# A graph attention and mixture-of-experts kernel: rows of x for 48 edge tiles fetched ahead of the table, edge lists loaded in rows

## The chip, the cores and the metric

The kernel runs on one core of one Trainium2 chip. The metric is the device time of one execution in microseconds (us). Four runs of the kernel before took 2566.82 to 2573.57 us, with a median of 2571.59 us.

## What is computed

There are 6250 nodes with 256 features and 206250 edges (two directions of 100000 random pairs, and one self-loop a node), sorted by destination. The first layer is graph attention with 8 heads of 32 features, the second a mixture of 16 experts, of which each node uses two.

```python
xn = layernorm(x)
hh = (xn @ W).reshape(n, 8, 32)
scores = leaky_relu((hh*a_src).sum(-1)[src] + (hh*a_dst).sum(-1)[dst], 0.2)
alpha = exp(scores - segment_max(scores, dst)[dst]);  alpha /= segment_sum(alpha, dst)[dst]
out = segment_sum(hh[src] * alpha[:, :, None], dst) + xn
x = x + elu(layernorm(out) * gamma + beta)
x = x + layernorm(y + moe(y)) * f_gamma + f_beta          # y = layernorm(x), top 2 of 16 experts
```

## The kernel before, in words

**The table.** The kernel first makes a table in DRAM with one row of 280 floats for every node: 8 heads of 32 features and a one each (264 floats), then two factors of the attention weight for each head (16 floats). x is held in 49 blocks of 128 nodes, all loaded ahead by SP (xs, L159) in batches of 2, 6, 8, 8, ... blocks. For each block TensorE turns the block (L294), ScalarE copies it out of PSUM (L296), TensorE multiplies it by W with the attention vectors folded in (wx, L299), ScalarE scales the product and takes two exponentials (L302 to L309), VectorE keeps the scores (sd, L310), and POOL stores the block's rows (L313). The normalization's statistics are VectorE's (L193, L194).

**The edge lists.** src and dst are cut into 52 chunks of 31 tiles of 128 edges (NK, CT). Before, edge e of a chunk stands on partition e // 31, in column e % 31, so that each partition reads 124 contiguous bytes for each chunk (L129 to L141). windows() (L242), traced ahead of the seventh batch, subtracts the first destination of a chunk from its destinations (dl), turns dl in 13 pieces on TensorE, which ScalarE casts to bytes (dlt, L260) and SP stores (dlb, L261), and takes the bounds of the distances.

**The edge loop.** The loop runs over the chunks, and in each over four groups of 8, 8, 8 and 7 tiles (GROUPS). For each tile POOL issues one indirect DMA that gathers 128 table rows by the source indices into a buffer hx (gather, L200 to L211). There are four such buffers of one group each. The first two groups are gathered right after the table (L316). For each group VectorE makes two matrices of zeros and ones (ohT L1022, oh L1029); TensorE multiplies ohT by the destinations' factors (pm, L1040); VectorE forms the weights (uv, L1064 to L1069) and multiplies the gathered rows by them (L1072); TensorE sums the rows into the chunk's destinations (agg, L1076). At the end of a chunk the sum is carried over (L1090 to L1095) and stored to accd, and a block of 128 finished nodes goes through node_block (L584): it loads a from accd and x, normalizes, applies the ELU, writes rest (L620) and computes the routing's logits (lg, L630).

**The experts.** When a round of blocks is complete (ROUNDS, five of them), routing() places its rows, POOL scatters every block's row twice (L830, out of ys, L816), and expert tiles of 128 rows are worked one per group, three groups (LAG) after the scatters: weights are loaded by SP, and TensorE multiplies (L881, L896). After the loop the open tiles are worked, and the results are fetched (L915), combined, normalized and stored.

**Order of work.** A scheduler puts each engine's instructions in a fixed order, by the place in the program and by estimated times. tc.issue_after(i) puts the block's instructions behind i on i's engine alone. Every engine works its own queue in order. POOL's queue holds the table stores, the gathers, the scatters and the result fetches; SP's holds the loads and some of the stores.

Of the kernel before, what the change touches and what calls it, by code (L numbers as in the profile page):

```python
# [36 lines left out]
def kernel(  # L37
# [89 lines left out]
    tp, tr = tail // CT, tail % CT  # L127

    def edge_list(eng, t, ap):  # L129
        eng.dma_start(  # L130
            t[:, : (NK - 1) * CT].rearrange("p (k g) -> p k g", g=CT),
            ap[0 : (NK - 1) * CE].rearrange("(k p g) -> p k g", p=P, g=CT),
        )
        o = (NK - 1) * CE
        if tp:
            eng.dma_start(t[:tp, (NK - 1) * CT : NT], ap[o : o + tp * CT].rearrange("(p g) -> p g", g=CT))
        if tr:
            eng.dma_start(
                t[tp : tp + 1, (NK - 1) * CT : (NK - 1) * CT + tr],
                ap[o + tp * CT : NE].rearrange("(p g) -> p g", p=1),  # L140
            )  # L141

    hxp = ctx.enter_context(tc.tile_pool(name="hxp", bufs=4))
    prep = ctx.enter_context(ExitStack())
    ed = prep.enter_context(tc.tile_pool(name="ed", bufs=1))
    dst_i = ed.tile([P, NT], I32, name="dst_i")
    nc.vector.memset(dst_i[:, (NK - 1) * CT :], N - 1)
    nc.vector.memset(src_sb[:, (NK - 1) * CT :], PADN)
    nc.vector.memset(src_sb[:, NT:], PADN)
    xs = ed.tile([P, NB, C], F32, name="xs")  # L150
    nc.vector.memset(xs[:, NB - 1, :], 0.0)
    batches = []
    while not batches or batches[-1][1] < NB:
        i = batches[-1][1] if batches else 0
        batches.append((i, min(NB, i + (2, 6, 8)[min(2, len(batches))])))
    for i, j in batches:
        n = min(j, NB - 1) - i
        if n:
            nc.sync.dma_start(xs[:, i : i + n, :], x[i * P : (i + n) * P, :].rearrange("(i p) c -> p i c", p=P))  # L159
    nc.sync.dma_start(xs[:LAST, NB - 1, :], x[(NB - 1) * P : N, :])  # L160
    wx = ed.tile([P, KC, C + 2 * H], F32, name="wx")
# [6 lines left out]
    nc.sync.dma_start(base_i[:, : NK - 1], dst[0 : (NK - 1) * CE].rearrange("(k e) -> e k", e=CE)[0:1, :])  # L168
    nc.sync.dma_start(base_i[:, NK - 1 :], dst[(NK - 1) * CE : (NK - 1) * CE + 1].rearrange("(k e) -> e k", e=1))
    edge_list(nc.sync, dst_i, dst)  # L170
    edge_list(nc.sync, src_sb, src)

# [5 lines left out]
    gg = row_of(g_gamma, C, "gg")  # L178
    gb = row_of(g_beta, C, "gb")
    fg = row_of(f_gamma, C, "fg")  # L180
    fb = row_of(f_beta, C, "fb")
    gtb = row_of(gate_b, E, "gtb")
    gw = const.tile([P, KC, E], F32, name="gw")
    nc.sync.dma_start(gw, gate_w.rearrange("(k p) e -> p k e", p=P))


    rest = const.tile([P, NB, C], F32, name="rest")
# [12 lines left out]
    def gather(k, g0, n):  # L200

        hx = hxp.tile([P, n, R], F32, name="hx")
        for g in range(n):
            c = k * CT + g0 + g
            t = nc.gpsimd.indirect_dma_start(  # L205
                out=hx[:, g, :],
                out_offset=None,
                in_=table[:, :],
                in_offset=bass.IndirectOffsetOnAxis(ap=src_sb[:, c : c + 1], axis=0),
            )  # L210
        return hx, t  # L211
# [5 lines left out]
    with tc.tile_pool(name="a1", bufs=1) as a1, tc.tile_pool(name="a3", bufs=3) as a3, tc.tile_pool(  # L217
        name="aps", bufs=4, space=bass.MemoryType.PSUM
    ) as aps:
# [22 lines left out]
        def windows():  # L242

            base_f = a1.tile([1, NK], F32, name="base_f")
            nc.vector.tensor_copy(base_f, base_i)
            bb = aps.tile([P, NK], F32, name="pxt")
            nc.tensor.matmul(bb, lhsT=ones[:1, :], rhs=base_f, start=True, stop=True)
            base_b = a1.tile([P, NK], F32, name="base_b")
            nc.vector.tensor_copy(base_b, bb)
            nc.vector.tensor_sub(down[:, : NK - 1], base_b[:, : NK - 1], base_b[:, 1:])  # L250
            nc.vector.tensor_copy(dl, dst_i)
            d3 = dl.rearrange("p (k g) -> p k g", g=CT)
            nc.vector.tensor_tensor(d3, d3, base_b[:, :, None].to_broadcast([P, NK, CT]), ALU.subtract)

            dlt = a1.tile([P, TR, P], U8, name="dlt")
            for i in range(TR):
                n = min(P, NT - i * P)
                pt = aps.tile([P, P], F32, name="pxt")
                nc.tensor.transpose(pt[:n, :], dl[:, i * P : i * P + n], ident)
                nc.scalar.copy(dlt[:n, i, :], pt[:n, :])  # L260
                nc.sync.dma_start(dlb[i * P : i * P + n, :], dlt[:n, i, :])  # L261
            b1r = a1.tile([E, F], F32, name="b1r")
            nc.scalar.dma_start(b1r, b1)
            b1t = a1.tile([P, E, FC], F32, name="b1t")
            for f in range(FC):
                pt = aps.tile([P, E], F32, name="pxt")
                nc.tensor.transpose(pt, b1r[:, f * P : (f + 1) * P], ident[:E, :E])
                nc.vector.tensor_copy(b1t[:, :, f], pt)
            nc.scalar.dma_start(b1d.rearrange("e p f -> p e f"), b1t)
            two = a1.tile([P, 2], F32, name="two")  # L270
            nc.vector.tensor_reduce(two[:, 0:1], dl, AX.X, ALU.max)
            nc.vector.tensor_reduce(two[:, 1:2], dl, AX.X, ALU.min)
            nc.vector.tensor_scalar(two[:, 1:2], two[:, 1:2], -1.0, float(P - 1), op0=ALU.mult, op1=ALU.add)
            pw = aps.tile([2, P], F32, name="pxt")
            nc.tensor.transpose(pw, two, ident)
            far = a1.tile([2, 1], F32, name="far")
            nc.vector.tensor_reduce(far, pw, AX.X, ALU.max)
            pf_ = a1.tile([1, 2], F32, name="pf_")
            pp = aps.tile([1, 2], F32, name="ph")
            nc.tensor.transpose(pp, far, ident[:2, :2])  # L280
            nc.vector.tensor_copy(pf_, pp)
            return base_f, pf_

        for q, (i0, i1) in enumerate(batches):
            if q == 6:
                base_f, pf_ = windows()
            for b in range(i0, i1):
                stats(a3, xs[:, b, :], st[:, b, :])
            inv_std(rstd[:, i0:i1], st[:, i0:i1, 1])
            nc.vector.tensor_scalar_mul(low[:, i0:i1], rstd[:, i0:i1], 0.2)  # L290
            for b in range(i0, i1):
                pt = aps.tile([P, KC, P], F32, name="pxt")
                for k in range(KC):
                    nc.tensor.transpose(pt[:, k, :], xs[:, b, k * P : (k + 1) * P], ident)  # L294
# [18 lines left out]
                nc.gpsimd.dma_start(table[b * P : (b + 1) * P, :], hr)  # L313


# [78 lines left out]

    def load(ap, lo_, hi_, engines=mybir.ALL_ENGINES, after=()):
# [8 lines left out]
    with tc.If(load(flag[:, 0:1], 0, 1) > 0):  # L404
        with tc.tile_pool(name="m1", bufs=1) as m1, tc.tile_pool(name="m2", bufs=2) as m2, tc.tile_pool(
# [6 lines left out]
            nc.vector.tensor_copy(dst_f[:, :NT], dst_i)  # L412
# [148 lines left out]
    with tc.tile_pool(name="w2", bufs=2) as w2_, tc.tile_pool(name="w3", bufs=3) as w3_, tc.tile_pool(  # L561
# [252 lines left out]
        def to_send(b):  # L814

            y = e2.tile([P, C], F32, name="ys", bufs=5)  # L816
# [227 lines left out]

        weighed = []
# [5 lines left out]
        for k in range(NK):  # L1051
            after = used[-2] if k > 1 else ()
            agg = wps.tile([P, RA], F32, name="agg")
            for g0, n in BOUNDS:
# [4 lines left out]
                hx, gathered = early.pop(0) if early else gather(k, g0, n)  # L1059
# [24 lines left out]
                some()  # L1084
                if g0 == 0:
# [96 lines left out]
```

## Time and profile before

| | us |
|---|---|
| median of 4 runs | 2571.59 (2566.82 to 2573.57) |
| the profiled execution | 2573.83 |
| its span, from the first to the last instruction | 2572.0 |
| first table store, last table store issued by POOL | 18.1, 87.9 |
| first and last table gather issued by POOL | 90.5, 2241.2 |
| POOL busy in gathers of the table, 1612 of them | 1543.0 |
| POOL busy in scatters and in result fetches, 98 each | 97.1, 97.1 |
| POOL busy in table stores, 49 | 26.7 |
| mean granted TensorE clock | 0.857 |

A busy time counts the instruction on its engine; the DMA that it starts moves its data later, and the wait for that stands with the instruction that needs the data. "Idle before" is the time in which an engine did nothing ahead of an instruction, and the releaser is what ended it. Durations are those of one execution under the profiler.

### The profile page before, as it was taken

What the parts mean: (1) busy time and instruction counts of PE and PEld (TensorE: products, weight loads), DVE (VectorE), ACT (ScalarE), POOL (GpSimd) and SP (SyncE); (2) the same over time, 40 slices, a digit from 0 to 9 for tenths busy, and PEclk for the clock granted to TensorE, in tenths of its full rate; (3) what the DMA queues carried; (4) which work ended last, traced back from release to release, by engine and by line L of the source; (5) the groups of instructions that cost most, each with busy time, mean ns of one, the idle gap of its engine ahead of it and who ended that gap; (6) DMA issues with size and microseconds to landing.
All of it is one profiled execution on the core that took longest, in us unless ns stands there. A gap on an engine that the chain in (4) does not pass through costs nothing.

```text
span 2572.0 us, 34571 instructions
## 1 busy us (share of the span) xinstructions
PE 1847.5 (72%) x10229; PEld 1552.4 (60%) x10229; DVE 1608.3 (63%) x3120; ACT 526.6 (20%) x1822; POOL 1765.0 (69%) x1866
## 2 busy tenths in 40 slices
PE   7365665655662679889847888867889868868985
PEld 6244454444451568778736777756778657756774
DVE  5476666666674666766747676665766846747802
ACT  6200000000000122222211222212222212224442
POOL 3577777777777777777777777777777777747202
PEclk9677778777876899899979999888889989979997
DMA  7555556555445588898857888877888878849995
GB/s 222 134 147 170 151 161 173 152 170 141 131 139 156 161 245 269 270 282 264 270 173 238 247 275 272 266 236 248 262 264 278 249 232 263 281 150 337 300 289 164
DMA packets 389306, 567.74 MB, mean 221 GB/s; under 512 B 102535, under 2 KB 278750, under 8 KB 389110
## 3 DMA queue, kind: packets, MB, share of 16 engines
q0 software_dynamic: 89904, 263.85, 34.6%
q1 hardware_dynamic: 257130, 264.89, 33.7%
q10 hardware_dynamic: 42076, 36.71, 4.2%
q8 instruction: 84, 1.38, 0.2%
q14 instruction: 112, 0.92, 0.1%
HBM read 497.58 MB, written 67.67 MB: 220 GB/s over the span
## 4 chain that ended last, share of the span: by engine, by line
PE 27%; POOL 22%; DMA 19%; DVE 13%; issue 12%; ACT 1%; DVEq 0%; POOLq 0%; SPq 0%; ACTq 0%
POOL hx L205 21%; PE agg L1076 12%; DMA hx<-table,src_sb 10%; PE po L896 6%; PE ph L881 5%; DVE hx L1072 4%; DMA out_dram<-o 4%; DMA xg<-ys,pos 2%; DMA accd<-carry 2%; DMA a<-accd 1%; DVE oh L1029 1%; PE pt L872 1%; DVE uv L1067 1%; PE pt L628 1%; DVE uv L1064 1%
## 5 line engine op out<-in xcount | busy, mean ns | idle before, releaser
L205 POOL DMA_INDIRECT hx<-table,src_sb x1612 | 1543.0, 957 | 500.7 <-issue 435.7
L1076 PE MATMUL agg<-hx,oh 128*128 128x264 f32 x3224 | 961.4, 455 | 402.8 <-DVE hx L1072 402.7
L1076 PEld LDWEIGHTS agg<-hx,oh 128*128 128x128 f32 x3224 | 698.1, 225 | 544.6 <-DVE hx L1072 416.0
L1072 DVE TENSOR_TENSOR hx<-hx,pm 128x2112 f32<-128x2112 f32 x208 | 474.4, 2281 | 4.2
L896 PE MATMUL po<-w2s,hT 128*128 128x256 f32 x1384 | 358.9, 399 | 90.3 <-ACT hT L890 89.8
L881 PEld LDWEIGHTS ph<-xt,w1s 128*128 128x128 f32 x2768 | 344.0, 195 | 23.3 <-issue 7.3
L896 PEld LDWEIGHTS po<-w2s,hT 128*128 128x128 f32 x1384 | 268.5, 200 | 142.9 <-ACT hT L890 104.6
L881 PE MATMUL ph<-xt,w1s 128*128 128x128 f32 x2768 | 350.1, 279 | 4.3 <-ACT xt L874 2.5
L1029 DVE TENSOR_TENSOR oh<-along,dl 128x1024 f32<-128x1024 f32 x208 | 245.5, 1180 | 23.0 <-PE agg L1076 22.9
L1022 DVE TENSOR_TENSOR ohT<-dlr,along 128x1024 bf16<-128x1024 uint8 x208 | 244.5, 1176 | 0.1
L890 ACT ACTIVATE hT<-ph,b1s 128x128 f32<-128x128 f32 x692 | 199.8, 366 | 213.9 <-PE ph L881 194.0
L915 POOL DMA_INDIRECT hx<-yg,pos x98 | 97.1, 990 | 173.5 <-DVE y L933 110.2
L1067 DVE TENSOR_TENSOR uv<-uv,hx 128x128 f32<-128x128 f32 x208 | 59.9, 288 | 248.1 <-DMA hx<-table,src_sb 215.6
L1064 DVE TENSOR_REDUCE uv<-pm 128x128 f32<-128x384 f32 x208 | 110.9, 533 | 84.6 <-PE pm L1040 84.4
L197 ACT ACTIVATE mv<-mv,eps 128x1 f32<-128x1 f32 x98 | 28.9, 294 | 628.4 <-DVE mv L194 628.4
L830 POOL DMA_INDIRECT xg<-ys,pos x98 | 97.1, 990 | 59.4 <-issue 50.8
L898 ACT COPY yr<-po 128x256 f32<-128x256 f32 x173 | 63.7, 368 | 335.9 <-PE po L896 317.7
L1040 PEld LDWEIGHTS <-ohT 128*128 128x128 bf16 x1612 | 71.5, 97 | 79.0 <-issue 33.9
L1040 PE MATMUL pm<-abw,ohT 128*128 128x48 bf16 x1612 | 74.9, 184 | 59.0 <-DVE ohT L1022 59.0
L594 DVE TENSOR_SCALAR den<-a 128x8 f32<-128x8 f32 x49 | 9.1, 185 | 167.3 <-DMA a<-accd 167.3
L874 ACT COPY xt<-pt 128x256 f32<-128x256 f32 x173 | 66.4, 384 | 159.5 <-PE pt L872 159.5
L817 DVE SCALAR_TENSOR_TENSOR ys<-rest,mv,fb 128x256 f32<-128x256 f32 x49 | 23.6, 482 | 112.6 <-DMA xg<-ys,pos 112.5
(204 smaller groups left out, 1329.8 us busy)
## 6 DMA issues: line engine op xcount, KB each, us to landing
w1s<-in_L_ffn_w_dram SPq DMA_DIRECT2D x173, 512.0 KB
w2s<-in_L_ffn_w_dram SPq DMA_DIRECT2D x173, 512.0 KB
hx<-table,src_sb POOLq DMA_INDIRECT x1612
dlr<-dlb SPq DMA_DIRECT2D x52, 496.0 KB
xr<-xg SPq DMA_DIRECT2D x173, 128.0 KB
yg<-yr ACTq DMA_DIRECT2D x173, 128.0 KB
xg<-zero SPq DMA_DIRECT2D x9, 1024.0 KB
accd<-carry ACTq DMA_DIRECT2D x52, 132.0 KB
```

The lines of the kernel that those rows point to most:

```text
L205: t = nc.gpsimd.indirect_dma_start(out=hx[:, g, :], out_offset=None, in_=table[:, :], in_offset=bass.IndirectOffsetOnAxis(ap=src_sb[:, c : ...
L830: t = nc.gpsimd.indirect_dma_start(out=xg[r][:, :], out_offset=bass.IndirectOffsetOnAxis(ap=pos[k][:n, b : b + 1], axis=0), in_=sent_rows[ ...
L881: marks["pe"] = nc.tensor.matmul(ph[:, f, :], lhsT=w1s[:, k, f * P : (f + 1) * P], rhs=xt[:, k, :], start=(k == 0), stop=(k == KC - 1),)
L890: marks["act"] = nc.scalar.activation(hT[:, f, :], ph[:, f, :], AF.Relu, bias=b1s[:, f : f + 1])
L896: marks["pe"] = nc.tensor.matmul(po, lhsT=hT[:, f, :], rhs=w2s[:, f, :], start=(f == 0), stop=(f == FC - 1))
L915: t = nc.gpsimd.indirect_dma_start(out=into[:n, k, :C], out_offset=None, in_=yg[parts[i][2]][:, :], in_offset=bass.IndirectOffsetOnAxis(ap ...
L1022: nc.vector.tensor_tensor(ohT, dlr[:, g0 : g0 + n, :], along[:, None, P:].to_broadcast([P, n, P]), ALU.is_equal,)
L1029: nc.vector.tensor_tensor(oh, along[:, None, :P].to_broadcast([P, n, P]), dl[:, k * CT + g0 : k * CT + g0 + n, None].to_broadcast([P, n, P ...
L1040: t = nc.tensor.matmul(pm[:, g * S3 : (g + 1) * S3], lhsT=ohT[:, g, :], rhs=abw, start=True, stop=True)
L1064: nc.vector.tensor_reduce(uv, pm[:, : n * S3].rearrange("p (n t h) -> p n h t", n=n, t=3), AX.X, ALU.add)
L1072: nc.vector.tensor_tensor(rows, rows, wt.unsqueeze(3).to_broadcast([P, n, H, D1]), ALU.mult)
L1076: t = nc.tensor.matmul(agg, lhsT=oh[:, g, :], rhs=hx[:, g, :RA], start=(g0 == 0 and g == 0), stop=(carry is None and g0 + g == CT - 1),)
```

## The change

Edges are laid out by rows: edge e of a chunk now stands in tile e // 128, on partition e % 128. Each list is loaded with one chunk in each partition, in two halves, into buffers of hx. The columns are turned on TensorE: turn_src casts up to 8 of a chunk's tiles to floats on VectorE, turns them and copies them into src_sb; it runs first for the first tile of each group, and for the other tiles ahead of batches 2 to 5. The distances of the destinations are formed in rows (away), stored to dlb from there in one DMA, and turned into dl after the last block, ahead of the early gathers.

With the first columns there, POOL fetches 128 rows of x for the first tile of groups 4 to 51, that is of chunks 1 to 12, into rest, which is not used otherwise at that time. These 48 tiles are not gathered from the table. In the loop, three groups ahead, TensorE turns the tile's x rows (raw_turn); two groups ahead it multiplies them by wx, and ScalarE writes the table row's values into the first tile of hx (raw_rows). VectorE takes the rows' statistics for a chunk's four tiles, one chunk ahead (raw_stats). Gathers are now traced two groups ahead of their use, behind the group's scatters, instead of at their use.

x is loaded in batches into three buffers, the load of batch q + 2 behind the first store of batch q. SP instead of POOL issues the table stores. Six loads of row vectors and gate weights are issued by SP behind the table stage. ys has three buffers instead of five. (A branch that these inputs do not take gets dst_f from dl instead of dst_i; that hunk is left out.)

```diff
-    xs = ed.tile([P, NB, C], F32, name="xs")
-    for i, j in batches:
-            nc.sync.dma_start(xs[:, i : i + n, :], x[i * P : (i + n) * P, :]...)
-    edge_list(nc.sync, dst_i, dst)
-    edge_list(nc.sync, src_sb, src)
+    HALVES = ((0, 16), (16, CT))
+    def edge_rows(ap, pad):
+        out = []
+        for lo, hi in HALVES:
+            t = hxp.tile([NK, (hi - lo) * P], I32, name="hx")
...
+            full = ap[: (NK - 1) * CE].rearrange("(k e) -> k e", e=CE)[:, lo * P : hi * P]
+            split = (NK - 1) // 16 * 16
+            nc.sync.dma_start(t[:split], full[:split])
+            nc.sync.dma_start(t[split : NK - 1], full[split:])
...
+            nc.sync.dma_start(t[NK - 1 : NK, :rest_of], ap[o : o + rest_of].rearrange("(a e) -> a e", a=1))
...
+    RAW = 48
+    RAW0 = len(GROUPS)
+    def fetch_rows(out, table_, c):
+        return nc.gpsimd.indirect_dma_start(
+            out=out, out_offset=None, in_=table_[:, :],
+            in_offset=bass.IndirectOffsetOnAxis(ap=src_sb[:, c : c + 1], axis=0),
+        )
+    def gather(k, g0, n, raw=False):
         hx = hxp.tile([P, n, R], F32, name="hx")
-        for g in range(n):
+        for g in range(int(raw), n):
+            t = fetch_rows(hx[:, g, :], table, k * CT + g0 + g)
         return hx, t
...
+        def x_rows(q):
+            i, j = batches[q]
+            t = ax.tile([P, 8, C], F32, name="xs")
...
+                if q > 2:
+                    order.enter_context(tc.issue_after(stores[batches[q - 2][0]].ins))
...
+                    nc.sync.dma_start(t[:, :n, :], x[i * P : (i + n) * P, :].rearrange("(i p) c -> p i c", p=P))
...
+        x_rows(0)
+        x_rows(1)
+        src_r = edge_rows(src, PADN)
+        x_rows(2)
+        dst_r = edge_rows(dst, N - 1)
+        def turn_src(gs):
...
+                    nc.vector.tensor_copy(sf[:, done : done + len(here), :], src_r[h][:, here[0] : here[-1] + 1 : d, :])
...
+            for i in range(len(gs)):
+                nc.tensor.transpose(pt[:, i, :], sf[:, i, :], ident[:NK, :NK])
+            nc.vector.tensor_copy(src3[:, :, gs[0] : gs[-1] + 1 : d].rearrange("p k g -> p g k"), pt)
...
         def windows():
-            nc.vector.tensor_copy(dl, dst_i)
-            nc.vector.tensor_tensor(d3, d3, base_b[:, :, None].to_broadcast([P, NK, CT]), ALU.subtract)
-            for i in range(TR):
-                nc.tensor.transpose(pt[:n, :], dl[:, i * P : i * P + n], ident)
-                nc.scalar.copy(dlt[:n, i, :], pt[:n, :])
-                nc.sync.dma_start(dlb[i * P : i * P + n, :], dlt[:n, i, :])
+            for i, n in enumerate(GROUPS):
+                part = away[:, g0 : g0 + n, :]
+                nc.vector.tensor_copy(part, dst_r[h][:, o : o + n, :])
+                nc.vector.tensor_scalar(part, part, first, None, op0=ALU.subtract)
+                nc.vector.tensor_copy(dlt[:, g0 : g0 + n, :], part)
+                for j, op in enumerate((ALU.max, ALU.min)):
+                    nc.vector.tensor_reduce(spread[:, i, j : j + 1], part, AX.XY, op)
+            nc.sync.dma_start(dlb[: NK * CT, :].rearrange("(k g) e -> k g e", g=CT), dlt)
...
+        turn_src(firsts)
+        rest = const.tile([P, NB, C], F32, name="rest")
+        for j in range(RAW):
+            k, i = divmod(RAW0 + j, len(GROUPS))
+            fetch_rows(rest[:, j, :], x, k * CT + firsts[i])
         for q, (i0, i1) in enumerate(batches):
+            if 2 <= q < 6:
+                g0 = firsts[q - 2]
+                turn_src(list(range(g0 + 1, g0 + GROUPS[q - 2])))
...
-                nc.gpsimd.dma_start(table[b * P : (b + 1) * P, :], hr)
+                stores[b] = nc.sync.dma_start(table[b * P : (b + 1) * P, :], hr)
+                if b == i0 and 0 < q < len(batches) - 2:
+                    x_rows(q + 2)
+        for i, n in enumerate(GROUPS):
...
+            for g in range(n):
+                nc.tensor.transpose(pt[:, g, :], away[:, g0 + g, :], ident[:NK, :NK])
+            nc.scalar.copy(dl.rearrange("p (k g) -> p k g", g=CT)[:, :, g0 : g0 + n].rearrange("p k g -> p g k"), pt)
...
-            y = e2.tile([P, C], F32, name="ys", bufs=5)
+            y = e2.tile([P, C], F32, name="ys", bufs=3)
...
+        def ahead(g):
+            k, i = divmod(g, len(GROUPS))
+            hxs[g] = gather(k, BOUNDS[i][0], BOUNDS[i][1], g in raws)
+        def raw_stats(k):
+            js = [g - RAW0 for g in range(k * len(GROUPS), (k + 1) * len(GROUPS)) if g in raws]
+            if js:
+                st = raw_st[:, js[0] : js[-1] + 1, :]
+                for j in js:
+                    stats(w2_, rest[:, j, :], raw_st[:, j, :])
+                inv_std(st[:, :, 0], st[:, :, 1])
+                nc.vector.tensor_scalar_mul(st[:, :, 1], st[:, :, 0], 0.2)
+        def raw_turn(g):
+            pt = wk.tile([P, KC, P], F32, name="pt")
+            for k in range(KC):
+                nc.tensor.transpose(pt[:, k, :], rest[:, g - RAW0, k * P : (k + 1) * P], ident)
+            xt = e2.tile([P, KC, P], F32, name="xt")
+            nc.scalar.copy(xt, pt)
+        def raw_rows(g):
...
+            for k in range(KC):
+                nc.tensor.matmul(ph, lhsT=xt[:, k, :], rhs=wx[:, k, :], start=(k == 0), stop=(k == KC - 1))
+            by_head = hx[:, 0, :RA].rearrange("p (h d) -> p h d", h=H)
+            nc.vector.memset(by_head[:, :, D:], 1.0)
+            nc.scalar.activation(by_head[:, :, :D], ph[:, :C]..., AF.Copy, scale=r1)
+            nc.scalar.activation(hx[:, 0, RA : RA + H], ph[:, C : C + H], AF.Exp, scale=r1)
+            nc.scalar.activation(hx[:, 0, RA + H :], ph[:, C : C + H], AF.Exp, scale=r2)
...
-                hx, gathered = early.pop(0) if early else gather(k, g0, n)
+                hx, gathered = hxs.pop(now)
...
                 some()
+                with ExitStack() as order:
+                    order.enter_context(tc.issue_after(sums[-1].ins))
+                    order.enter_context(tc.issue_after(weighed[-1].ins))
+                    if g0 == 0:
+                        raw_stats(k + 1)
+                    if now + 2 < NK * len(GROUPS):
+                        ahead(now + 2)
+                    if now + 2 in raws:
+                        raw_rows(now + 2)
+                    if now + 3 in raws:
+                        raw_turn(now + 3)
```

## The prediction

> **What bounds the kernel now.** I first read the busy line of the page and its POOL row over the 40 slices, then the stretches of 100 us, then the single line that fills POOL, and last the waits of DVE. By the first line PE is busiest:
>
> ```profile
> PE 1847.5 (72%) x10229; PEld 1552.4 (60%) x10229; DVE 1608.3 (63%) x3120; ACT 526.6 (20%) x1822; POOL 1765.0 (69%) x1866
> ...
> POOL 3577777777777777777777777777777777747202
> ```
>
> No engine looks full. But POOL's row is a flat 7 from the third slice to the 36th, whatever PE and DVE do. The stretches (columns: length, then busy time and instructions of PE, PEld, DVE, ACT, POOL, the granted clock, DMA share, GB/s) show the same:
>
> ```profile
> 290.00:390.00 100.00, 63.75 (x268) 50.41 (x269) 71.47 (x117) 7.09 (x21) 75.83 (x80) 0.74 0.54 151
> 790.00:890.00 100.00, 41.51 (x204) 33.27 (x204) 47.46 (x77) 9.86 (x26) 75.94 (x79) 0.68 0.53 158
> 1090.00:1190.00 100.00, 88.45 (x547) 77.74 (x545) 69.41 (x108) 23.88 (x82) 75.92 (x80) 0.93 0.89 278
> ```
>
> POOL starts 80 instructions in every 100 us, so one per 1.25 us, with PE at 41 or at 88. The missing quarter is in the answer on the gather's line L205 (minimum, median, maximum of one; then the idle time ahead of it):
>
> ```profile
> L205 POOL DMA_INDIRECT hx<-table,src_sb x1612: 940/946/1714, 90.5 to 2241.2; - x180
> ...
>   issue: 435.7, 1430
> ```
>
> Each gather takes 0.95 us, and 0.30 us (435.7/1430) before it in which POOL waits for nothing shown. From 90.45 to 2242.4 POOL issues 1612 gathers and 86 of the 98 scatters: 1698 x 1.25 = 2122 of 2152 us. **POOL's issue rate is the bound of the edge loop.** Before 90.45 POOL issues only 49 table stores (26.7 us). After it, expert tiles on PE end the run; their number still open when the loop ends is fixed by the count of groups, not by time, so I keep that tail as it is.
>
> **What goes.** 48 of the 1612 table gathers leave the loop, one in each group of chunks 1 to 12: 48 x 1.25 = **-60.0 us**. POOL also loses the 49 stores, which is worth nothing in the loop: they were in front of it.
>
> **What comes before the loop.** The 48 fetches of x rows cost POOL the same 1.25 us each (scatters and result fetches of 256 columns take 0.99), 60 us, and must fit ahead of the first table gather, which waits for the last store:
>
> ```profile
> 87.90 0.54 POOL L313 DMA_DIRECT2D table<-hr  x1 [1.06 <-ACT hr L309]
> ...
> 90.45 1.02 POOL L205 DMA_INDIRECT hx<-table,src_sb  x1 [2.02 <-DMA table<-hr]
> ```
>
> They need the first four columns of src. The source rows stand on SP behind 1.0 MB of x, with 0.5 MB of weights beside them: 2.3 MB at the 278 GB/s of the first 20 us is 8.3 us, plus 3.7 us that the first x load took to land: 12 us. Two casts, four transposes and a copy bring it to 14 to 18. So the raw fetches end at 74 to 78, 12 us ahead of 90.45: hidden. If that cover goes, each us past 90.45 costs one.
>
> The table stage itself: blocks pass PE four per 5.08 us (24.48 to 29.56), of which PE works 4.97, so PE paces it. It gains 31 transposes of src and loses 13 of dl: at 1.04 us for 8 (L294), 18 x 0.13 = +2.3. The 13 casts to dlt leave ACT (276 ns, -3.6). DVE gains 15 us (casts of 3968 elements a row three times at L251's 0.62 ns, one subtraction and two reductions at L253's 1.13 ns, 1612 elements out of PSUM, less 6.5 removed), beside 44.9 busy in the first 80 us; as x now comes in batches, statistics can no longer run ahead to 38 us as they did. Stores queue on SP with the x loads of later batches: 1 MB takes 3.8 us at 278 GB/s, against six buffers of 1.27 us a block. The edge lists lose 13,056 rows of 124 bytes (two lists, 51 chunks, 128 partitions). The weights may come earlier than the 9.2 us of before, as only part of x is ahead of them. Bounds -6 to +10; I take **0**, since the terms cancel within their errors.
>
> By the Trainium skill (GPSIMD Engine Reference, 1. Specifications) POOL shares its SBUF interfaces with VectorE and contends with two-port modes and with two SBUF inputs, which speaks against putting gathers beside the casts. The trace has one such meeting and one without loss:
>
> ```profile
> 95.56 1.01 POOL L205 DMA_INDIRECT hx<-table,src_sb  x1 [0.30 <-issue]
> ...
> 96.79 0.97 DVE L347 TENSOR_TENSOR abt<-abt,ab 128x784 f32<-128x784 f32 x1
> 96.87 1.71 POOL L205 DMA_INDIRECT hx<-table,src_sb  x1 [0.30 <-issue]
> ```
>
> If by that rule each of some 20 casts and subtractions held a fetch by the 0.77 us of this row, the raw fetches would end 15 us later, and 3 us would show; by the other 0.07 us row nothing would.
>
> **Between table and loop.** 31 transposes of away (4.0 us) and four ACT copies stand ahead of the maximum over sd (pe, L326), and six row loads (3 us on SP) may stand ahead of the first fetch of dlr. POOL already waits 4.28 + 4.22 us here for chunk 0 (125.44 and 138.07), so a later chunk 0 shows: 0 to +7, I take **+3**.
>
> **Inside chunks 1 to 12.** A chunk is now 27 gathers, 33.75 us instead of 38.75. Is DVE quick enough? Its waits in ten chunks, 193 to 581 (in total, times, longest):
>
> ```profile
> DVE uv L1067 <- DMA hx<-table,src_sb: 71.7, 23, 6.8
> DVE lg L630 <- PE pt L628: 26.4, 10, 3.3
> DVE den L594 <- DMA a<-accd: 21.4, 8, 3.7
> ```
>
> Of 388 us DVE is busy 259.6 and waits 71.7 + 5.8 at uv for rows. Without these a chunk is 31.0 us of DVE, some 5 us of it the other waits. Added per chunk: four statistics (0.42 + 0.09 each), four small memsets (0.06 each) and one multiplication (0.16): 2.4 us. That is **33.4 against 33.75**: POOL stays the bound by a hair, with no slack. PE gains two transposes (0.26) and four matmul passes (0.98, by 3.93 for 16) a group, 5 us a chunk, on 23 busy. ACT gains a copy and three activations (1.4 us) a group on 2.4 a chunk. They hide in PE's and ACT's idle time, but PE and ACT work in order: the new matmuls stand ahead of the next sums, the transposes ahead of pt of the node block, so lg waits longer. Bounds 0 (the hair holds) to 2 us a chunk, 24; I take 0.75, **+9**, as lg and den are the nearest rows and each now costs 2 to 3 a chunk.
>
> **Scatters.** ys has 3 buffers instead of 5. A block's two scatters take 2.53 us and land in 2.4. A third buffer freed at that point leaves POOL 5.2 us of issued work, and DVE needs 0.48, ACT 0.51. That is enough until DVE does a group in between: 833.01 to 838.36 is a gap of 5.35 between two ys, so ready after 6.5, a stall of 1.3. Some 22 groups hold the first four rounds' 86 scatters: 0 to +30; DVE was waiting at ys then (24.5 us before 817), and POOL never for it, so I take a quarter: **+7**. The order gather ahead of scatter shifts by one group on POOL; with four buffers each gather still waits for the same sum, so I cost it at nothing; what covers it is the three groups between scatter and first load of the tile.
>
> **Sum.** -60.0 + 0 + 3 + 9 + 7 = -41. The profiled execution took 2573.8 (span 2572.0), so 2532.8; the runs' median lies 2.2 below, so **2531**.
>
> **Rivals.**
> - *Nothing is given back*: statistics, waits and ys all hide. For: 33.4 is below 33.75, DVE waits at ys. Against: no slack. -60, and the table up to 6 earlier: 2505 to 2518. Chance 0.20.
> - *DVE, or ys, takes POOL's place*: 2 us a chunk and 1.3 a group, +24 + 29, less 60: 2560 with the fill; cases from 2545 to 2566. For: 5 us of order-bound waits a chunk. Chance 0.15.
> - *Slower, by ACT's order*: xt and the three activations of a raw tile stand on ACT behind the node block's inv_std, which waits for DVE:
>
> ```profile
> L197 ACT ACTIVATE mv<-mv,eps 128x1 f32<-128x1 f32 x20 | 5.9, 295 | 218.5 <-DVE mv L194 218.5
> ```
>
>   That is 10.9 us a time, twice a chunk. uv of the group then waits for ACT, and PE's sums behind the raw matmul. One such block a chunk not hidden makes it 33.4 + 10.9 = 44.3, 5.6 more than 38.75, and 12 chunks +67: 2640. It decides from 38.75 - 33.4 = 5.4 us a chunk. Against: the rows are turned two to three groups (17 us) ahead, and a buffer's round (8.4 of gathers, 3 to land, 8 of work) leaves 14 us of four groups' 33.75. Chance 0.15.
> - *It does not do what it says*: src comes late, the fetches end 30 us or more after the table, and with the 9 and 7 above nothing is left: within 5 us of before. Chance 0.05; smaller delays are in the forecast.
>
> The forecast (2518 to 2545) has 0.45. About 0.2%, 5 us, is what a measurement of this kernel can tell from no change. Faster is 0.45 + 0.20 + 0.15 = 0.80, the same 0.05, slower 0.15. The range 2507 to 2572 leaves out the slower case and the outermost of the rest.
>
> **What would show it.** Right: 1564 gathers on L205 and 48 of rest, these from about 16 to 78 us; the first table gather within 6 us of 90; POOL at 80 per 100 us again from there on; the loop's last gather near 2200. Wrong: POOL idle ahead of L205 waiting for agg in chunks 1 to 12 (DVE or ACT is the bound there: look at uv's wait, for ACT or for rows); POOL idle ahead of L830 for ys; a first table gather past 96; more expert tiles left after the loop.

## The result, and the profile after

The kernel after takes **2566.64 us** (median of 48 runs, 2555.71 to 2575.86), the kernel before 2571.37 beside it: a ratio of **0.9982**, 95% interval 0.9976 to 0.9989. It is 4.7 us faster, where 41 were forecast. (The two profiled executions, from which the rows below come, differ by 7.3 us.)

The busy line of the page after, POOL's row, and the two stretches that answer to those of before:

```profile
PE 1890.7 (74%) x10567; PEld 1587.0 (62%) x10567; DVE 1645.8 (64%) x3307; ACT 584.3 (23%) x2029; POOL 1739.3 (68%) x1817
...
POOL 4457777777777777777777777777777767746202
```

```profile
290.00:390.00 100.00, 69.05 (x350) 54.98 (x348) 77.87 (x163) 19.68 (x72) 75.89 (x80) 0.88 0.59 167
790.00:890.00 100.00, 49.93 (x246) 40.25 (x247) 57.28 (x92) 12.51 (x33) 75.93 (x80) 0.73 0.53 162
```

POOL's row shows the loss: the flat 7 begins in the fourth slice instead of the third (a slice is 64 us). From there on POOL again issues 80 instructions in 100 us, so chunks 1 to 12 run at POOL's rate. The answer on the gather's line, now L183, and three rows of POOL's timeline (start, length, engine, line, what; in brackets the idle time before it and its releaser):

```profile
L183 POOL DMA_INDIRECT hx<-table,src_sb x1564: 942/946/1338, 121.1 to 2228.6; - x196
...
L183 POOL DMA_INDIRECT rest<-in_x_dram,src_sb x48: 942/946/1300, 28.9 to 89.8; - x48
```

```profile
88.58 0.95 POOL L183 DMA_INDIRECT rest<-in_x_dram,src_sb  x1 [0.30 <-issue]
89.83 0.94 POOL L183 DMA_INDIRECT rest<-in_x_dram,src_sb  x1 [0.30 <-issue]
121.11 1.26 POOL L183 DMA_INDIRECT hx<-table,src_sb  x1 [30.33 <-DVE top L395]
```

The 48 gathers are gone and the 48 fetches are done at 90.8, but the table is not: POOL then stands idle for 30.33 us. The profile puts the end of this wait down to VectorE (top), which comes last, at 120.8; the last table store had left SP only at 118.3, the end of this row of SP's timeline:

```profile
89.22 29.08 SPq L363 DMA_DIRECT2D table<-hr  x16
```

In the two profiled executions (spans 2572.0 and 2564.7):

| stretch | before | after | difference |
|---|---|---|---|
| start to first table gather | 90.5 | 121.1 | +30.7 |
| first to last table gather | 2150.7 | 2107.5 | -43.2 |
| last table gather to the end | 330.8 | 336.1 | +5.3 |

The loop's -43.2 is -60 (48 x 1.25), +8.4 in POOL's waits ahead of the first chunks (16.9 us against 8.5 in before), +6.5 in one wait for agg near the loop's end that before does not have, and some 2 more. The wait for agg is there without the fetches too (6.3 us in e17 below), so they are not its cause.

**Where the table stage is late.** Blocks whose second exponential ACT has started by a given time, counted in the traces:

| kernel | 30 us | 40 | 50 | 60 | 80 | 100 | first table gather |
|---|---|---|---|---|---|---|---|
| before | 10 | 18 | 25 | 33 | 43 | 49 | 90.5 |
| after | 6 | 9 | 9 | 17 | 29 | 40 | 121.1 |

Sixteen blocks are lost before 50 us, at some 1.5 us a block (the 24 left of before take 36 us). VectorE's timeline of after shows where some seven of them go (an estimate: 10.3 us at 1.5 a block):

```profile
37.76 1.28 DVE L297 CAST away<-hx 52x1024 f32<-52x1024 int32 x2
38.96 1.46 DVE L298 TENSOR_SCALAR away<-away,first 52x1024 f32<-52x1024 f32 x2
40.35 0.74 DVE L299 CAST dlt<-away 52x1024 uint8<-52x1024 f32 x1
41.02 2.32 DVE L301 TENSOR_REDUCE spread<-away 52x1 f32<-52x1024 f32 x2
43.27 0.67 DVE L299 CAST dlt<-away 52x1024 uint8<-52x1024 f32 x1
43.87 2.33 DVE L301 TENSOR_REDUCE spread<-away 52x1 f32<-52x1024 f32 x2
46.12 1.21 DVE L297 CAST away<-hx 52x1024 f32<-52x1024 int32 x2
47.26 0.87 DVE L298 TENSOR_SCALAR away<-away,first 52x1024 f32<-52x1024 f32 x1
48.05 0.35 DVE L360 TENSOR_SCALAR sd<-ph,rstd 128x16 f32<-128x16 f32 x2
```

The work on the destinations stands in one pile from 37.76 to 51.4. The copies sd, which free the PSUM buffers of blocks that ACT had finished by 38.2, stand behind it. TensorE's waits show the price (in all, times, longest):

```profile
PE ph L349 <- DVE sd L360: 11.8, 1, 11.8
```

The fetches themselves start at 28.9 instead of 14 to 18 for the same reason: the second cast of src columns (L243, at 27.14) stands on VectorE behind four sd copies that each waited for ACT (the first for 4.69 us).

### The profile page after: what moved, and what is told of

It is laid out like the page before. It is cut to its first block, busy times and chain, and to the rows that moved or that the text cites. A ratio compares the mean times of both kernels' runs of the same rounds, so it can differ in the third digit from the quotient of the medians.

```text
span 2564.7 us, 35777 instructions
## 1 busy us (share of the span) xinstructions
PE 1890.7 (74%) x10567; PEld 1587.0 (62%) x10567; DVE 1645.8 (64%) x3307; ACT 584.3 (23%) x2029; POOL 1739.3 (68%) x1817
## 4 chain that ended last, share of the span: by engine, by line
PE 25%; DMA 20%; POOL 16%; issue 11%; DVE 9%; ACT 1%; DVEq 0%; SPq 0%; ACTq 0%; POOLq 0%
POOL hx L183 14%; DMA hx<-table,src_sb 11%; PE agg L1196 10%; PE po L971 6%; PE ph L956 6%; DVE hx L1192 3%; DMA out_dram<-o 3%; DMA xg<-ys,pos 2%; DMA accd<-carry 2%; POOL xg L905 1%; DMA a<-accd 1%; PE pt L947 1%; DVE uv L1187 1%; ACT hT L965 1%; DVE uv L1184 1%
## 5 line engine op out<-in xcount | busy, mean ns | idle before, releaser
L183 POOL DMA_INDIRECT hx<-table,src_sb x1564 | 1496.8, 957 | 529.0 <-issue 415.8
L1196 PE MATMUL agg<-hx,oh 128*128 128x264 f32 x3224 | 931.2, 445 | 313.1 <-DVE hx L1192 308.7
L1196 PEld LDWEIGHTS agg<-hx,oh 128*128 128x128 f32 x3224 | 679.9, 219 | 450.7 <-DVE hx L1192 319.7
L956 PE MATMUL ph<-xt,w1s 128*128 128x128 f32 x2768 | 355.4, 282 | 5.2 <-ACT xt L949 5.0
L176 ACT ACTIVATE mv<-mv,eps 128x1 f32<-128x1 f32 x98 | 28.9, 294 | 457.6 <-DVE mv L173 422.7
L1115 PEld LDWEIGHTS <-ohT 128*128 128x128 bf16 x1612 | 71.7, 97 | 87.4 <-issue 42.8
L892 DVE SCALAR_TENSOR_TENSOR ys<-rest,mv,fb 128x256 f32<-128x256 f32 x49 | 23.7, 484 | 149.3 <-DMA xg<-ys,pos 146.0
L698 PE MATMUL pt<-ident,y 128*128 128x128 f32 x98 | 23.5, 329 | 86.4 <-DVE pm L1189 46.7
```

Of the source, the lines that this page charges most:

```text
L183: return nc.gpsimd.indirect_dma_start(out=out, out_offset=None, in_=table_[:, :], in_offset=bass.IndirectOffsetOnAxis(ap=src_sb[:, c : c + ...
L956: marks["pe"] = nc.tensor.matmul(ph[:, f, :], lhsT=w1s[:, k, f * P : (f + 1) * P], rhs=xt[:, k, :], start=(k == 0), stop=(k == KC - 1),)
L1115: t = nc.tensor.matmul(pm[:, g * S3 : (g + 1) * S3], lhsT=ohT[:, g, :], rhs=abw, start=True, stop=True)
L1196: t = nc.tensor.matmul(agg, lhsT=oh[:, g, :], rhs=hx[:, g, :RA], start=(g0 == 0 and g == 0), stop=(carry is None and g0 + g == CT - 1),)
```

## The experiments

Two theories of the table stage. **Order**: queues worked in order (VectorE's pile, SP's loads and stores) hold the blocks. **Contention**: the fetches take the DMA engines from loads and stores. For the fill, the time from the end of the table to a steady loop, the theory is a wait for buffers. Seven runs were on a chip on which before takes 2571 us; eight (e1 to e4, e12 to e15) fell on two other chips, on which before takes 3080 to 3082, so some kernels were run again. Each ratio is to before on the same chip. "After" itself was not run on the other chips.

**Without the fetches** (e17_no_raw3; e14_no_raw2 and e1_no_raw on the other chips).

```diff
-    RAW = 48
+    RAW = 0
```

> The kernel after with no rows of x fetched ahead: all 1612 tiles are gathered from the table, the rest is as after (edge lists in rows, x in batches, stores on SP). Two theories for the table stage, which ends 30.7 us later in the kernel after (first table gather at 121.1 instead of 90.45). Order theory: engines that work in order hold the blocks (VectorE's pile of destination work from 37.8 to 51.3 us, SP held 15.7 us by a memset), so without the fetches the first table gather still comes at 110 to 121 us, and the time is the 2566.6 of after plus 60 for the 48 gathers, less up to 10: 2616 to 2627. Contention theory: the 6.3 MB of the fetches crowd out the loads of x and the stores, so without them the first table gather comes at 85 to 97 and the time is 2595 to 2605.

> The kernel after without its 48 fetches: all 1612 tiles are gathered from the table, the edge lists are still loaded in rows and turned, x in batches, stores on SP. Order theory: the table stage is late without the fetches too, first table gather at 111 to 118, and the time is the 60 us above the kernel after less 3 to 8: 2619 to 2625, ratio 1.018 to 1.021. Contention theory: first table gather at 90 to 100, and 2597 to 2607, ratio 1.010 to 1.014.

> The kernel after without its 48 fetches, again on a chip with the times of the case. Order theory: first table gather at 111 to 118, 2619 to 2625, ratio 1.018 to 1.021. Contention theory: first table gather at 90 to 100, 2597 to 2607, ratio 1.010 to 1.014.

e17: 2618.81, ratio 1.0179 (1.0153 to 1.0205), first table gather 113.4, 9 blocks at 50 us as in after, and the same wait of PE for sd:

```profile
PE ph L349 <- DVE sd L360: 11.6, 1, 11.6
```

So **23.0 of the 30.7 us are there without a single fetch**; the fetches' part is the rest, 7.7. The start lies where the order theory put it, the time just below its 2619. That all of the 23.0 are order is not shown by this run: the new layout's work and x in batches are in it too. From the first to the last gather e17 takes 2169.5 and after 2107.5: 62.0 for 60 us of gathers, so the work on the fetched rows in chunks 1 to 12 gives nothing back. e14: 3101.58, ratio 1.0072 (1.0049 to 1.0095), first table gather 113.4. e1: 3099.83, 1.0052 (1.0032 to 1.0073), 112.5. Both starts agree with the order theory; both ratios are below 1.018, but the loop on those chips has other waits beside POOL's rate (in e14 POOL waits 186.7 us for agg, and 217.9 for what the profile calls remote).

**Thin fetches** (e9_thin).

```diff
+        nc.gpsimd.memset(rest[:, :RAW, 16:], 0.0)
-            fetch_rows(rest[:, j, :], x, k * CT + firsts[i])
+            fetch_rows(rest[:, j, :16], x, k * CT + firsts[i])
```

> The kernel after, whose 48 fetches ahead of the table bring 16 of the 256 columns of a row (the other columns are set to zero by POOL in its idle first microseconds, so these 48 tiles' features are left out of the result). POOL issues as much as before, DMA moves 6.3 MB less and DVE, SP, PE and ACT have the same order. Contention theory (the fetched rows fill the DMA engines from 30 to 90 us, so table stores and x loads land late): the first table gather comes at 90 to 100 us instead of 121. Order theory (SP's queue with stores, x loads and edge lists in order, and DVE's pile of destination work hold the blocks): it still comes at 113 to 121. Time by the first 20 to 30 us below the kernel after, by the second within 8 us of it.

2561.67, ratio 0.9957 (0.9937 to 0.9976), first table gather 115.8. Start and time lie in the order theory's ranges. The bytes that are left out (5.9 MB by the two traces) are worth 5.3 us of start, the rest of the fetches another 2.4 against e17. On this chip contention is real and is the small part.

**The destination work in pieces, the padding early** (e10_all, e18_all3; e2_memset_pool, e4_pieces and e15_all2 on the other chips).

```diff
-                nc.vector.memset(t[:, rest_of:], pad)
+                nc.gpsimd.memset(t[:, rest_of:], pad)   # e2, e10; e15, e18: ahead of wa on VectorE
+                if 2 <= q < 6 and b == i0 + 5:
+                    with tc.issue_after(kept.ins):       # e4, e10, e15, e18: behind that block's sd
+                        piece(q - 2)                     # one of the four groups of windows()
```

> The kernel after with the padding of the edge rows written by POOL instead of VectorE. Order theory: SP's wait of 15.7 us for that memset goes, the stores start when the first block is ready, and the first table gather comes 5 to 15 us earlier than 121.1, the time falls by as much: 2552 to 2562. If only VectorE's pile counts, or under the contention theory: within 3 us of after, 2564 to 2570.

> The kernel after with the destination work of the four groups of tiles traced behind the sixth block of batches 2 to 5, one group each and pinned behind that block's score copy on VectorE, instead of all at the seventh batch. Order theory: TensorE's wait of 12 us for VectorE at 36 to 48 us goes, first table gather at 105 to 114, the time falls by 7 to 15: 2552 to 2560. Contention theory: blocks are late by the loads of x anyway; first table gather 118 to 123, 2563 to 2570.

> The kernel after with three edits of order: the free space of the gap kernel, the padding of the destination lists set by POOL instead of late on DVE, and the destination work cut in four pieces that stand on DVE behind blocks of batches 2 to 5. Order theory: the first table gather comes at 95 to 108 us, and the time is 13 to 25 us below the gap kernel's, ratio 0.983 to 0.988. Contention theory: the first table gather stays at 113 or later and the time within 6 us of the gap kernel's.

> The kernel after with the free space, the destination work in four pieces, and the padding of the destination list set ahead of VectorE's work on the attention vectors, at some 6 us instead of 29 (in the kernel with padding on POOL it still came at 30.2, behind the first fetch in POOL's order). If SP's wait for the padding is what keeps the table from 113.7 us to an earlier start: first table gather at 100 to 108 and 6 to 13 us below that kernel. If it is not, first table gather at 111 to 115 and the same time within 3 us.

> The kernel of e15_all2 again on a chip with the times of the case: the kernel after with the free space, the destination work in pieces and the padding at 6 us. If SP's wait for the padding holds the table (113.7 us in e10_all): first table gather at 100 to 108, 2536 to 2543. If not: 111 to 115, 2546 to 2552.

e10 (with the free space of e8 below): 2548.91, 0.9915 (0.9891 to 0.9940), first table gather 113.7. That misses the order theory: it had the table at 95 to 108 and a ratio of 0.983 to 0.988, and the start is the one that the contention theory allowed (113 or later). Against e8 the pieces bring 7.3 us of start and 6.6 of median time (the runs of the two overlap); 15 blocks are done at 50 us instead of the 9 of after, and 49 at 110 us instead of 44. Its padding came at 30.2, since POOL's order put it behind the first fetch. e18 set it early: 2548.72, 0.9910 (0.9892 to 0.9928), 114.7. So that SP's wait for the padding, 15.7 us in after, holds the table is **not** borne out. The test is not a clean one: in e18 the earlier casts of src cost early blocks (2 at 30 us, the first at 27.0 instead of 21.8 in e10). On the other chips: e2 3095.43, 1.0049 (1.0024 to 1.0074), first table gather 159.3; e4 3102.1, 1.0063 (1.0037 to 1.0090), 160.3; e15 3092.22, 1.0036 (1.0009 to 1.0064), 163.2. None of these starts is one that either theory expected. Without the fetches the first table gather comes at 112.5 and 113.4 there (e1, e14), and with them at 154.1 in e3 below, which has the table stage of after. So on those chips the fetches are the larger part, and these three runs decide nothing about the order.

**The old edge lists with the fetches** (e11_before_raw; e16_spread2, and e12_spread on another chip). These start from before and add only the fetches, the raw rows in the loop, gathers two ahead, stores on SP, and three ys buffers; x and the lists are loaded as before.

```diff
+        if q == 2:                                       # e11: src behind two batches of x
+            edge_list(nc.sync, src_sb, src)
-                nc.gpsimd.dma_start(table[b * P : (b + 1) * P, :], hr)
+                stored = nc.sync.dma_start(table[b * P : (b + 1) * P, :], hr)
+                with tc.issue_after(stored.ins):         # e12, e16: x and lists in parts
+                    for job in due.get(b, []):           # behind single stores
+                        job()
```

> The kernel before with only the core of the change: 48 fetches of rows of x ahead of the table, turned into table rows in chunks 1 to 12, gathers two groups ahead, table stores on SP, ys with three buffers; x is loaded all ahead as before, the edge lists are loaded as before (src behind the second batch of x) and are not turned. Order theory: raw fetches from 15 to 22 us, first table gather at 88 to 97, fill as before, loop 60 shorter: ratio 0.976 to 0.982. Contention theory: the same fetches beside the stores hold the table until 105 to 120: ratio 0.985 to 0.991.

> The kernel before_raw with SP's queue written out by hand: src of chunks 0 to 12 right behind the second batch of x, x three batches ahead of the stores, dst in 8 pieces and the rest of src in 6 pieces behind single table stores; fetches, raw rows and loop as in before_raw, in which the first table store left SP only at 45.65 us, behind all of x and both lists. Order theory: 8 to 10 blocks are done at 30 us instead of 6, the table stage runs at the pace of before beside the 48 fetches, first table gather at 90 to 98, time 12 to 20 us below before_raw: ratio 0.980 to 0.985. Contention theory (the fetches beside x and the stores hold the blocks, wherever they stand in the queue): first table gather at 105 or later, ratio 0.987 to 0.991.

> The kernel of e12_spread again, on a chip with the times of the case, since on the other chip engines stood for some 10 us at a time on nothing that the profile shows while the fetches ran. Order theory: table stage at the pace of before beside the 48 fetches, first table gather at 90 to 98, ratio to before 0.980 to 0.985. Contention theory: first table gather at 105 or later, ratio 0.987 to 0.991.

e11: 2543.94, 0.9894 (0.9871 to 0.9917), but first table gather 110.1. SP's timeline (issues; the second number is how long the issue held the queue) shows why:

```profile
32.72 12.47 SPq L136 DMA_DIRECT2D dst_i<-in_dst_dram  x1
...
45.65 3.88 SPq L314 DMA_DIRECT2D table<-hr  x7
```

One list of 124-byte pieces holds SP for 12.47 us, and the first store stands behind it. With six buffers for rows the blocks stop at 6 until stores are out, and 8 are done at 50 us. Start and ratio lie in the contention theory's ranges, though the rows show an order. e16 breaks that order: 9 blocks at 30 us, 22 at 50, first table gather **99.8**, 2542.54, ratio 0.9882 (0.9864 to 0.9901). With all fetches and bytes in place 21 of the 31 us are back; beside the 9.3 left stand VectorE's waits for x (10.5 us) and ACT's for stores (6.0). The start lies between the two theories; the ratio misses the order theory's 0.980 to 0.985 and lies in the contention theory's 0.987 to 0.991. In the trace the start is 9.3 us late instead of at most 7.5, and the stretch behind the last gather is 335.1 against 330.8. But that execution, at 2535.07, is the fastest of six and 7.5 us below their median, so where the other runs lose these 7.5 is not known; and although e16 starts 10.3 us earlier than e11, its median is only 1.4 below.

e12, the same kernel on another chip: 3075.31, ratio 0.9978 (0.9956 to 1.0000), first table gather 149.3, outside both theories (see the last section).

**The fill** (e8_gap2; e3_gap on another chip).

```diff
+            spare = gap.tile([P, 11000], F32, name="spare")   # 43 KB in the branch not taken
             ext2 = m1.tile([P, 2, NK], F32, name="ext2")
```

> The kernel after with a spare tile of 43 KB in the branch that is not taken, so that the branch's tiles lie on other addresses; no instruction of the path that runs is added. Theory for the late first chunk: the first load of abw waits for all 24 gathers ahead of the branch to land (155.9 us), because its buffer lies where the branch has buffers of gathers. Then the first ohT comes at 141 to 148 instead of 161.8, POOL's waits ahead of the first chunks fall from 23.4 to some 8 us, and the time falls by 10 to 16: 2551 to 2557. If the loads wait for something else (the abd store, the branch itself): no change, 2564 to 2569. The table's end stays at 121 by both.

> The kernel after, with 43 KB left free ahead of the buffers of the branch that is not taken, so that the buffers of the first abd rows (abw) no longer lie where that branch's gather buffers lie. If the fill behind the table is late because the first load of abw waits for all 24 early gathers to land (fill theory): the first abw load follows the abd store by 10 to 13 us instead of 26.7, POOL's idle time ahead of the first chunks falls from 23.4 to 8 to 12 us, and the time by 10 to 16: a ratio to the kernel before of 0.992 to 0.995. If something else holds the fill (the distances turned late, the row loads on SP): the wait only changes its name and the ratio stays at 0.997 to 0.999.

2555.53, ratio 0.9930 (0.9906 to 0.9954): 11.1 us below after, with one tile that nothing uses. SP's rows in after and in e8:

```profile
129.22 0.39 SPq L410 DMA_DIRECT2D abd<-ab  x1
155.89 0.37 SPq L1069 DMA_DIRECT2D abw<-abd  x1
```

```profile
129.39 0.39 SPq L410 DMA_DIRECT2D abd<-ab  x1
139.60 0.37 SPq L1073 DMA_DIRECT2D abw<-abd  x1
```

In after the first load of abw waits 26.7 us behind its data, until the gathers placed ahead of the branch have landed; in e8 it waits 10.2, as in before (98.79 to 108.87). The likeliest reason, which no run shows by itself, is that the big x tile that the change removed had kept the branch's gather buffers clear of abw's memory. POOL's waits ahead of the first chunks fall from 16.9 to 6.2 (the 23.4 of the texts above holds the 6.5 near the loop's end too). e3: 3080.59, 0.9992 (0.9968 to 1.0015), the first abw load 12.0 behind, first table gather 154.1.

**Three ys buffers alone** (e13_ys3, on another chip).

```diff
-            y = e2.tile([P, C], F32, name="ys", bufs=5)
+            y = e2.tile([P, C], F32, name="ys", bufs=3)
```

> The kernel before with three buffers for ys instead of five and nothing else. The prediction took +7 us of 0 to 30 for this: ratio 1.0027, up to 1.011. The trace after shows POOL waiting 5.0 us in all for ys, so by it the ratio is 1.000 to 1.002.

3078.16, ratio 0.9989 (0.9966 to 1.0012): no difference there. On the case's chip this was not run; in after POOL waits 5.0 us in all for ys, where in before it waited 5.5 for earlier scatters.

## Why the prediction was wrong

- **What comes before the loop: the step that failed.** It took 0, within -6 to +10; it was +30.7. It added the new work of each engine to its busy time (15 us on VectorE beside 44.9 of 80) and found room. It did not ask what stands behind that work in an engine's queue: 10.3 us of it in one piece (37.76 to 48.05) hold the sd copies, those hold PSUM, and TensorE stops. It also gave the x that now comes in batches no price. e17 gives 23.0 to the new layout and order, e9 5.3 to the bytes of the fetches, and 2.4 are left for the rest of them; the pile's part is 7.3 (e10 against e8). "The weights may come earlier" was the other way too: the second product with the attention vectors starts at 11.73 instead of 10.54, and the first table block's copy xt at 19.11 instead of 14.31.
- **The fetches hidden:** right in effect, by luck. They start at 28.9 instead of 14 to 18 and end at 90.8 instead of 74 to 78, past the 90.45 that was to cover them; the table is later still.
- **Between table and loop:** +3 taken, +8.4 measured, outside 0 to +7. The wait is none of those named; it came from memory laid out anew (e8).
- **What goes:** -60.0 was right (80 issues in 100 us; 62.0 between e17 and after).
- **Inside chunks 1 to 12:** POOL stays the bound, as said, but not by a hair, and the +9 was 0. Between 193 and 581 us VectorE is busy 311.7 us, and uv still waits 47.7 + 6.0 us for rows (71.7 + 5.8 in before). Worked as in the prediction, with 388 us as 11.5 chunks of 33.75, that is 29.1 us a chunk, not 33.4: of the waits counted into 33.4, lg's fell from 26.4 to 15.4 and den's from 21.4 to 1.6.
- **Scatters:** +7 taken; POOL's waits for ys and for earlier scatters are 5.0 us in after and 5.5 in before, so nothing is left of it.
- **The tail "as it is":** +5.3 in after; it is 330.7 to 339.6 in the kernels run on this chip, and what moves it is not known.
- **The rivals.** Inside the loop "nothing is given back" was right. "DVE or ys" and "slower, by ACT's order" did not occur. "Within 5 us of before" came true by another mechanism than the one priced at 0.05: the table was late, not the fetches. In "DVE or ys" a sum is wrong: before less 60, plus 24 + 29 and the fill's 3, is 2568, not 2560.
- **The clock,** which the prediction left out: at 290 to 390 us it was granted at 0.88 instead of 0.74, and one product of agg takes 461 ns there instead of 528. So TensorE's busy time rose only from 63.75 to 69.05 of 100 us, with 350 products and transposes instead of 268.

What stays open: how the 23 us of e17 divide further. The pile is 7.3 (e10 against e8), the old layout in a good order has 9.3 with fetches (e16); the rest, some 16, was not separated, and the parts need not add. The traces name one candidate that no run changed alone, the loads of x that now stand behind stores. VectorE's waits for them in the table stage, in after and in e17:

```profile
DVE s L172 <- DMA xs<-in_x_dram: 9.6, 3, 4.1
```

```profile
DVE s L172 <- DMA xs<-in_x_dram: 5.8, 2, 3.7
```

In before it waits 1.4 us for x in all. Counted by the second exponential, the 10th block is 22.4 us later than in before in after and 13.5 in e10, so the pieces win 8.9 there; but from the 25th block to the 40th e10 falls back from 14.8 to 23.6, and VectorE waits for x twice in that stretch (4.9 and 2.8 us). The wait of 6.0 to 6.5 us near the loop's end, in after, e8, e16 and e17 alike, was not tried.

## What to carry to other kernels

When work moves off the bound engine into an earlier stage, look at that stage as closely as at the bound: not whether busy times fit, but what stands behind each new instruction in its queue, and which buffer that holds. A tile added or removed moves other tiles; look for buffers that come to lie over memory with transfers still under way, even in a branch that is never taken. And make the parts alone: the fetches without the new layout (e11, e16) are 23 to 29 us below both kernels on this chip, and 7 below before on another (e12).

## What the runs showed of the hardware

**The other chips.** Up to the first table gather they match the case's chip as long as no fetch runs: 90.0 in e13 against 90.5 in before, 113.4 in e14 and in e17. With the fetches the table waits until 149.3 (e12) where this chip has 99.8 (e16, the same kernel). DMA queues from 30 to 70 us, in e16 and then in e12 (packets, MB, share of the engines):

```profile
q1 hardware_dynamic: 14979, 7.11, 63.3%
q0 software_dynamic: 1612, 4.40, 35.0%
q8 instruction: 2, 0.03, 0.3%
q14 instruction: 4, 0.03, 0.2%
```

```profile
q0 software_dynamic: 1592, 4.35, 38.0%
q1 hardware_dynamic: 1187, 1.19, 8.6%
```

POOL's fetches move as much on both; beside them the loads and stores of the other engines move 7.11 MB on the one and 1.19 on the other, though the DMA engines there are busy less than half of the time. The Trainium skill (DMA: Bandwidth & Descriptors, Queues, rings and completion order) says that a DMA engine takes turns between its queues packet by packet. No run here shows whether unequal turns are the reason: in these 40 us SP issued 24 table stores, three loads of x and the pieces of the lists in e16, but three stores and no load in e12, so the hardware queue of e12 had little to move. What the trace of e12 shows is that the engines stood still. This row of TensorE's waits holds one of 33.9 us, until 64.6, for nothing that the profile shows:

```profile
PE ph L318 <- issue: 37.0, 3, 33.9
```

In e12 the queues that the profile calls instruction moved no packet between 18.1 and 80.4 us; in e16 they moved six from 30 to 70. Whether that is part of the cause is not shown: TensorE's wait ends ahead of the next such packet. On those chips a change that puts gathers beside other work is worth less.

**Gathers beside VectorE.** While POOL fetches, VectorE works through its pile without a break. POOL's rows, to be held against VectorE's rows in the section on the result:

```profile
40.89 1.02 POOL L183 DMA_INDIRECT rest<-in_x_dram,src_sb  x1 [0.30 <-issue]
42.22 0.95 POOL L183 DMA_INDIRECT rest<-in_x_dram,src_sb  x1 [0.31 <-issue]
43.47 1.30 POOL L183 DMA_INDIRECT rest<-in_x_dram,src_sb  x1 [0.30 <-issue]
45.07 0.95 POOL L183 DMA_INDIRECT rest<-in_x_dram,src_sb  x1 [0.31 <-issue]
```

Fetches that start beside a reduction take 0.94 to 0.95 us, those that start beside a cast or a subtraction 1.02 to 1.30. The ten that start from 37.8 to 51.4 us take 1.2 us more than ten of 0.946. So there is a loss, of at most 0.35 us a meeting where the prediction weighed 0.77, and all 48 fetches lose 2.2. The rule on shared interfaces (the Trainium skill, GPSIMD Engine Reference, 1. Specifications) names VectorE's two-port modes and instructions with two SBUF inputs; the trace does not show in which mode a cast runs. The loss cost nothing here, since the table came later than the fetches.
